# A selective-scan block on one core: sixteen copies of the B and C rows, last states that enter through the first token, and a shifted order of the next step's pieces

## The chip, the cores and the metric

The kernel runs on one core of a Trainium2 chip. The core has five engines that run their own instruction streams: TensorE (PE in the profile), VectorE (DVE), ScalarE (ACT), GpSimd (POOL) and SyncE (SP), which here only issues DMA transfers; 16 DMA engines move the data. The metric is the device time of one execution in microseconds. Before the change it is 13002.54 us, the median of three runs (12999.16 to 13004.72).

## The reference

Two images of 96 channels and 128 x 128 positions pass through two layers. Nearly all the work is in the first layer's mixer: four Mamba scans over the 16384 positions, in row order, reversed row order, column order and reversed column order. Cut to what matters, one direction is:

```
xc, z = split(x @ in_w.T)                       # 192 channels each
xc    = silu(causal_conv4(xc) + conv_b)
dt_raw, Bm, Cm = split(xc @ xproj_w.T)          # 6, 16 and 16 rows
dt    = softplus(dt_raw @ dt_w.T + dt_b)
for t in positions:                             # h: 192 channels x 16 states
    h = exp(dt[t] * A) * h + dt[t] * Bm[t] * xc[t]
    y[t] = sum over the states of h * Cm[t]
out   = ((y + Dp * xc) * silu(z)) @ outp_w.T
```

Bm and Cm have 16 rows each per position, common to all 192 channels of a direction. The four outputs are fused by a 1x1 product and added to x. After that come a quantized feed-forward part, a 3x3 convolution and a second feed-forward part, which the change doesn't touch.

## The kernel before

For each image three stages follow each other: `normalize` (layer norm, written to DRAM in row order and in column order), `mamba` (the four scans) and `ffn_and_conv`. The change is in `mamba` alone.

**Tiling.** Directions are taken in two pairs (`PAIRS`), first the two forward ones, then the two reversed. A pair has 2 x 192 = 384 channels, which make three groups `g` of 128 partitions: group 0 belongs to the first direction, group 2 to the second, and group 1 is half and half (partitions 0..63 first, 64..127 second). A *step* is one pair and one block of T = 512 positions; there are 2 x 32 steps per image, 128 in all. A step has 24 *units*: for each of three groups, eight pairs of states (`s`, `s+1`). The loop variable `k` counts units through all steps of an image, and in the text "unit 12" is the twelfth of its step.

**A unit.** ScalarE makes two decay tiles `da` = exp(dt * A) in PSUM (`decay`, L330, two units ahead). GpSimd multiplies the B rows by `dtu` = dt * xc in place (`b_part`, L324, also two units ahead; it covers two states at once, 1024 elements a partition). VectorE runs the recurrence over the 512 positions of each state (`scan`, L334), which starts from the state that the step before left in `hst`. It then multiplies the result by the C rows in one instruction of 1024 elements (L409). TensorE adds the products up over the states, as matrix products with the identity into `y` (`sums`, L341). ScalarE keeps the last column of `h` in `hst` (L410). VectorE's order is: first scan of unit k, product of unit k-1, second scan of unit k. At the first unit of a group the finished `y` of the group before is multiplied by silu(z) (`gated`, L349).

**Rows on all partitions.** A scan on 128 partitions needs each B and C row on every partition. `rows_out` (L258 to L261) copies B and C of a step from PSUM to SBUF (64 rows, on partitions 32 to 95, in the order B of the first direction, B of the second, C of the first, C of the second) and writes them to DRAM as `bcd`, in `COPIES` = 4 copies. `row_tile` (L312 to L321) then fetches four rows at a time, spread over the partitions by an access pattern with repeats, 8 KB a partition and 1 MB in all. For group 1 these are two transfers, one for each half of the partitions. A tile serves two units. There are four buffers for B and three for C, so that a transfer is issued when an older tile is done with: B for units k+6 and k+7 at the top of each even unit k (the buffer was read last by the scans of unit k-1), and C for units k+4 and k+5 at its end (read last by TensorE's sums of unit k-1). SyncE issues all transfers in the order of the program.

**Pieces of the next step.** While a step is scanned, the input of the next is prepared by small functions in `prologue`: `load`, three `conv` and `conv_out`, the silu of `xc`, three `gate` and `gate_out`, the silu of `sz`, `rows` and `rows_out`, and for each group the chain `dt_in`, `dt_exp`, `dt_ln`, `dt_q`, `dt_log`, `dt_sum`, `dt_u` (softplus by parts; `dt_q` to `dt_u` are four GpSimd operations of 512 elements, L287 to L297). Each has a place (unit, 0 or 1): 0 is ahead of the unit's first scan, 1 at its end. The list `at` holds these places. All engines run in the order in which the program issues (`manual_schedule`), so a piece that waits holds up everything behind it on its engine. The pieces' PSUM tile `misc` has one buffer.

Of the kernel before, what the change touches and what calls it, by code (L numbers as in the profile page):

```python
# [10 lines left out]
F32 = mybir.dt.float32  # L11
# [3 lines left out]
AF = mybir.ActivationFunctionType  # L15
ALU = mybir.AluOpType
# [7 lines left out]
T = 512  # L24
NT = L // T
R = T // W
S = 16
# [2 lines left out]
HID = 384  # L30
PAIRS = ((0, 2), (1, 3))
NG = 3
COPIES = 4
B_AHEAD = 3
C_AHEAD = 2
AHEAD = 2
# [1 line left out]
BCO = 32  # L38
NBC = 4 * S
# [3 lines left out]
def tile_metaformer(ctx: ExitStack, tc: tile.TileContext, a: dict, out: bass.AP):  # L43
# [139 lines left out]
    def mamba(acc, xnr, xnc):  # L183

        with ExitStack() as st:
# [3 lines left out]
            rows_d = pool("rows_d", 3, space=DRAM)  # L189

            hst = one.tile([128, NG, S], F32, name="hst")
            acc_w = acc.rearrange("c (h w) -> c w h", w=W)

            def misc():
# [15 lines left out]
            def prologue(pi, i, d):  # L210

                rev = pi == 1
                lo = L - (i + 1) * T if rev else i * T
                src = []

                def load():
                    for n, dram in (("xa", xnr), ("xb", xnc)):
                        t = io.tile([C, T + 3], F32, name=n)
                        if i == 0:
                            nc.gpsimd.memset(t[:, T : T + 3] if rev else t[:, 0:3], 0.0)  # L220
                            nc.sync.dma_start(t[:, 0:T] if rev else t[:, 3 : T + 3], dram[:, lo : lo + T])
                        else:
                            nc.sync.dma_start(t, dram[:, lo : lo + T + 3] if rev else dram[:, lo - 3 : lo + T])
                        src.append(t[:, ::-1] if rev else t)
                    d["dt"], d["dtu"], d["yg"] = [], [], []

                def conv(g):
                    d["ps"] = inproj(pi, g, lambda dd, k, lo, hi: inx[:, dd, k, lo:hi], src, (0, 1, 2, 3))

                def conv_out(g):  # L230
                    if g == 0:
                        d["xc"] = two.tile([128, NG, T], F32, name="xc")
                    nc.scalar.activation(d["xc"][:, g, :], d["ps"], AF.Identity, bias=convb[:, pi, g : g + 1])  # L233

                def gate(g):
                    d["ps"] = inproj(pi, g, lambda dd, k, lo, hi: inz[:, dd, lo:hi], src, (3,))

                def gate_out(g):
                    if g == 0:
                        d["sz"] = two.tile([128, NG, T], F32, name="sz")  # L240
                    nc.scalar.copy(d["sz"][:, g, :], d["ps"])

                def silu(name):
                    nc.scalar.activation(d[name], d[name], AF.Silu)
                    nc.scalar.preload_act_table_set("natural_log_exp_and_others")

                def rows():

                    d["ps"] = misc()
                    for g in range(NG):  # L250
                        nc.tensor.matmul(
                            d["ps"][0 : BCO + NBC, :], bcw[:, pi, g, :], d["xc"][:, g, :], start=g == 0, stop=g == NG - 1
                        )

                def rows_out():

                    d["rows"] = one.tile([BCO + NBC, T], F32, name="rows")
                    nc.scalar.copy(d["rows"], d["ps"][0 : BCO + NBC, :])  # L258
                    d["bcd"] = rows_d.tile([COPIES, 2, NBC // 2, T], F32, name="bcd")
                    for n in range(COPIES):  # L260
                        nc.sync.dma_start(d["bcd"][n].rearrange("k r t -> (k r) t"), d["rows"][BCO:, :])  # L261

                def dt_in(g):
                    d["ps"] = misc()
                    w = dtw[:, pi, g * 128 : (g + 1) * 128]
                    nc.tensor.matmul(d["ps"], w, d["rows"][0 : 2 * RK, :], start=True, stop=True)  # L268

                def dt_exp(g):  # L270
                    bias = dtb[:, pi, g : g + 1]
                    d["e"] = one.tile([128, T], F32, name="e")
                    nc.scalar.activation(d["e"], d["ps"], AF.Abs, bias=bias)
                    dt = gen.tile([128, T], F32, name="dt")
                    nc.scalar.activation(dt, d["ps"], AF.Relu, bias=bias)  # L275
                    nc.scalar.activation(d["e"], d["e"], AF.Exp, scale=-1.0)
                    d["dt"].append(dt)

                def dt_ln(g):
                    d["q"] = one.tile([128, T], F32, name="q")  # L280
                    nc.scalar.activation(d["q"], d["e"], AF.Identity, bias=1.0)
                    d["ln"] = one.tile([128, T], F32, name="ln")
                    nc.scalar.activation(d["ln"], d["q"], AF.Ln)
                    nc.scalar.activation(d["q"], d["q"], AF.Identity, bias=minus_one[:, 0:1])

                def dt_q(g):
                    nc.gpsimd.tensor_tensor(d["q"], d["e"], d["q"], ALU.subtract)  # L287

                def dt_log(g):
                    nc.gpsimd.tensor_tensor(d["ln"], d["ln"], d["q"], ALU.add)  # L290

                def dt_sum(g):
                    nc.gpsimd.tensor_tensor(d["dt"][g], d["dt"][g], d["ln"], ALU.add)  # L293

                def dt_u(g):
                    dtu = gen.tile([128, T], F32, name="dtu")
                    nc.gpsimd.tensor_tensor(dtu, d["dt"][g], d["xc"][:, g, :], ALU.mult)  # L297
                    d["dtu"].append(dtu)


                at = [(0, 0, load), (8, 1, partial(silu, "xc")), (14, 1, partial(silu, "sz"))]
                at += [(12, 0, rows), (12, 1, rows_out)]
                for g, k in enumerate((4, 5, 6)):
                    at += [(k, 0, partial(conv, g)), (k, 1, partial(conv_out, g))]
                for g, k in enumerate((7, 10, 11)):
                    at += [(k, 0, partial(gate, g)), (k, 1, partial(gate_out, g))]
                for g, k in enumerate((13, 18, 21)):
                    pieces = (0, 0, dt_in), (0, 1, dt_exp), (1, 1, dt_ln), (2, 0, dt_q), (3, 0, dt_log), (3, 0, dt_sum), (4, 0, dt_u)
                    at += [(k + m, where, partial(f, g)) for m, where, f in pieces]
                return sorted(at, key=lambda p: p[:2])  # L310

            def row_tile(d, g, s, k, ahead):  # L312

                t = gen.tile([128, 4, T], F32, name=f"row{k}", bufs=ahead + 1)
                for half in range(2) if g == 1 else (slice(None),):
                    rows = slice(half * 64, half * 64 + 64) if g == 1 else half
                    at = s + S * (half if g == 1 else g // 2)
                    n = (64 if g == 1 else 128) // COPIES
                    src = d["bcd"][None, :, k, at : at + 4, :].broadcast_to((n, COPIES, 4, T))
                    nc.sync.dma_start(t[rows], src)  # L320
                return t  # L321

            def b_part(d, g, b):
                nc.gpsimd.tensor_tensor(b, d["dtu"][g][:, None, :].broadcast_to((128, 2, T)), b, ALU.mult)  # L324

            def decay(pi, d, g, s):

# [2 lines left out]
                    nc.scalar.activation(da[:, j, :], d["dt"][g], AF.Exp, scale=amat[:, pi, g, s + j : s + j + 1])  # L330
                return da

            def scan(i, g, s, j, da, b, h):
                nc.vector.tensor_tensor_scan(  # L334
                    h[:, j, :], da[:, j, :], b[:, j, :],
                    0.0 if i == 0 else hst[:, g, s + j : s + j + 1], ALU.mult, ALU.add,
                )

            def sums(s, y, c):
                for j in range(2):  # L340
# [34 lines left out]
            def later(k, where, f, *args):  # L375
                todo.setdefault((k, where), []).append(partial(f, *args))
# [14 lines left out]
            def feed(k):  # L391
                if k < total:
                    n = k // nu
                    b_part(state[n], units[k % nu][0], bs[k])

            def feed_decay(k):
                if k < total:
# [38 lines left out]
            for k in range(total + 6):  # L436
                n, u = divmod(k, nu)
                if u == 0 and n + 1 < len(steps):
                    for m, where, f in prologue(*steps[n + 1], state[n + 1]):
                        later(k + m, where, f)  # L440
                if k % 2 == 0:
                    fetch(k + 2 * B_AHEAD, 0, B_AHEAD, bs)
                feed(k + AHEAD)
                issue(k, 0)
                if k < total:
                    (_, i), (g, s) = steps[n], units[u]
                    da, b = das.pop(k), bs.pop(k)
                    hs[k] = b if (g, s) in BY_POOL else da
                    scan(i, g, s, 0, da, b, hs[k])
                if 0 < k <= total:  # L450
                    behind(k - 1)
                if k < total:
                    scan(i, g, s, 1, da, b, hs[k])
                if k % 2 == 0:
                    fetch(k + 2 * C_AHEAD, 1, C_AHEAD, cs)
                feed_decay(k + AHEAD)
# [166 lines left out]
```

## Time and profile before

| What | us |
|---|---|
| span of the profiled execution | 13002.5 |
| scan stage of the first image (168.2 to 5932.9) | 5764.7 |
| scan stage of the second image (6660.5 to 12423.2) | 5762.7 |
| VectorE busy in each of them | 5489 |
| GpSimd busy in each | 4500 |
| ScalarE busy in each | 3864 |
| TensorE busy in each | 4816, 4806 |

The busy time of an engine over a stage tells how full it is; it doesn't tell which wait ends last. For that, the groups of instructions have a second time, the idle time of the engine ahead of them, and the engine or transfer that ended it. The waits of SyncE tell when a buffer became free for a transfer: 4676.5 us on TensorE's sums for the C tiles and 2049.5 us on the scans for the B tiles. The DMA queue moved 3394 MB, of which the row tiles are 24 MB a step; 512 transfers write `bcd`, 128 KB each, and they land 9.8 us after their issue in the median. A row transfer of 1 MB lands after 7.5 us in the median, one of 512 KB after 8.0.

### The profile page before, as it was taken

Reading aid. Unit: us, or ns where it says so; the run is one execution under the profiler, and the core shown is the slowest. Engines: PE = TensorE matmul, PEld = TensorE weight load, DVE = VectorE, ACT = ScalarE, POOL = GpSimd, SP = SyncE. Lnnn points to the kernel's source line nnn. Section 1 sums busy time; section 2 is a strip of 40 time slices with the busy share of each in tenths; the row PEclk is TensorE's granted clock in tenths of the full one; section 3 lists DMA queues with packets and bytes.
Section 4 is the critical chain, followed back from the end, with each engine's and each line's share of the span. In section 5 each row is a group of like instructions: output and inputs, shape, how many; then the busy total and the mean of one; then the engine's idle time right before and its main releaser. Section 6 shows DMA issues by size and latency. Waiting matters only on the chain. (4 is left out here: it accounts for less than half of the span.)

```text
span 13002.5 us, 97992 instructions
## 1 busy us (share of the span) xinstructions
PE 10850.3 (83%) x24208; PEld 3987.1 (31%) x24208; DVE 11569.1 (89%) x10865; ACT 8560.0 (66%) x14738; POOL 9215.4 (71%) x4772
## 2 busy tenths in 40 slices
PE   6888888888888888888978888888888888888889
PEld 2323233333333333333323333332333333333233
DVE  5999999999999999995459999999999999999954
ACT  6666666666666666665566666666666666666655
POOL 4877778777787787772147778777787777877721
PEclk8999999999999999999989999999999999999999
DMA  7999999999999999992079999999999999999920
GB/s 226 287 294 282 298 288 285 295 283 298 288 285 295 283 295 289 285 295 68 13 226 285 298 283 292 290 285 298 285 291 291 284 298 286 290 294 281 296 61 13
DMA packets 545331, 3400.40 MB, mean 262 GB/s; under 512 B 81612, under 2 KB 82732, under 8 KB 146840
## 3 DMA queue, kind: packets, MB, share of 16 engines
q1 hardware_dynamic: 544760, 3394.12, 83.1%
q8 instruction: 195, 3.19, 0.1%
q14 instruction: 376, 3.08, 0.1%
HBM read 3288.94 MB, written 104.86 MB: 261 GB/s over the span
## 5 line engine op out<-in xcount | busy, mean ns | idle before, releaser
L324 POOL TENSOR_TENSOR row<-dtu,row 128x1024 f32<-128x1024 f32 x3072 | 7175.7, 2358 | 1739.3 <-DMA row<-bcd 1419.2
L334 DVE TENSOR_TENSOR_SCAN da<-da,hst,row 128x512 f32<-128x512 f32 x5952 | 7339.4, 1274 | 351.2 <-ACT da L330 194.6
L341 PE MATMUL y<-row,ident 128*128 128x512 f32 x12288 | 6120.1, 626 | 1113.3 <-DVE row L409 1098.9
L330 ACT ACTIVATE da<-dt,amat 128x512 f32<-128x512 f32 x6144 | 4249.4, 692 | 207.5 <-ACT hst L410 0.4
L341 PEld LDWEIGHTS y<-row,ident 128*128 128x128 f32 x12288 | 2288.9, 197 | 4779.4 <-DVE row L409 2292.3
L409 DVE TENSOR_TENSOR row<-da,row 128x1024 f32<-128x1024 f32 x3072 | 3705.9, 1206 | 19.6 <-DMA row<-bcd 18.8
L410 ACT COPY hst<-da 128x2 f32<-128x2 f32 x3072 | 484.0, 158 | 2235.5 <-DVE row L409 2233.3
L416 PE MATMUL y<-xc,dmat 128*128 128x512 f32 x768 | 526.1, 773 | 779.1 <-DVE sz L349 779.1
L287 POOL TENSOR_TENSOR q<-e,q 128x512 f32<-128x512 f32 x384 | 488.0, 1271 | 821.8 <-ACT hst L410 709.1
L233 ACT ACTIVATE xc<-misc,convb 128x512 f32<-128x512 f32 x384 | 264.2, 688 | 1117.5 <-PE misc L207 1117.5
L207 PE MATMUL misc<-xa,inx 96*128 96x512 f32 (+1 forms) x2048 | 932.4, 597 | 59.0 <-DMA xa<-xnr 57.2
L207 PE MATMUL misc<-xb,inx 96*64 96x512 f32 (+1 forms) x2048 | 928.1, 595 | 1.6 <-ACT xc L233 1.6
L531 POOL TENSOR_TENSOR acc<-acc,y 96x512 f32<-96x512 f32 x128 | 147.6, 1153 | 987.0 <-DVE y L530 987.0
L541 PE MATMUL pc<-pad,kw 96*96 96x512 f32 x1152 | 566.7, 593 | 0.0
L207 PEld LDWEIGHTS misc<-xa,inx 96*128 96x128 f32 (+1 forms) x2048 | 323.6, 163 | 625.5 <-issue 493.4
L293 POOL TENSOR_TENSOR dt<-dt,ln 128x512 f32<-128x512 f32 x384 | 486.9, 1268 | 30.1
L297 POOL TENSOR_TENSOR dtu<-dt,xc 128x512 f32<-128x512 f32 x384 | 488.5, 1272 | 0.5
L290 POOL TENSOR_TENSOR ln<-ln,q 128x512 f32<-128x512 f32 x384 | 488.1, 1271 | 0.5
L359 PE MATMUL misc<-sz,gmat 128*96 128x512 f32 x1024 | 483.6, 594 | 0.0
L416 PEld LDWEIGHTS y<-xc,dmat 128*128 128x128 f32 x768 | 129.0, 211 | 1102.1 <-DVE sz L349 1099.1
L268 PE MATMUL misc<-rows,dtw 12*128 12x512 f32 x768 | 439.7, 652 | 18.5 <-ACT dt L275 17.2
L132 DVE TENSOR_TENSOR xq<-xm,rs 96x512 fp8e5<-96x512 f32 x128 | 87.9, 687 | 387.8 <-ACT rs L128 387.8
(75 smaller groups left out, 8403.8 us busy)
## 6 DMA issues: line engine op xcount, KB each, us to landing
row<-bcd SPq DMA_DIRECT2D x2048, 1024.0 KB, 7.5
row<-bcd SPq DMA_DIRECT2D x2048, 512.0 KB, 8.0
bcd<-rows SPq DMA_DIRECT2D x512, 128.0 KB, 9.8
xa<-xnr SPq DMA_DIRECT2D x124, 193.1 KB, 5.8
xb<-xnc SPq DMA_DIRECT2D x124, 193.1 KB, 5.5
acc<-in_x_dram SPq DMA_DIRECT2D x16, 768.0 KB, 17.8
xnr<-xn SPq DMA_DIRECT2D x16, 768.0 KB, 4.3
xnc<-stg SPq DMA_DIRECT2D x16, 768.0 KB, 5.6
```

The source lines that it names most:

```text
L207: nc.tensor.matmul(ps[rows, :], w(PAIRS[pi][d], k, lo, hi), src[d][:, k : k + T], **se)
L287: nc.gpsimd.tensor_tensor(d["q"], d["e"], d["q"], ALU.subtract)
L290: nc.gpsimd.tensor_tensor(d["ln"], d["ln"], d["q"], ALU.add)
L293: nc.gpsimd.tensor_tensor(d["dt"][g], d["dt"][g], d["ln"], ALU.add)
L297: nc.gpsimd.tensor_tensor(dtu, d["dt"][g], d["xc"][:, g, :], ALU.mult)
L324: nc.gpsimd.tensor_tensor(b, d["dtu"][g][:, None, :].broadcast_to((128, 2, T)), b, ALU.mult)
L330: nc.scalar.activation(da[:, j, :], d["dt"][g], AF.Exp, scale=amat[:, pi, g, s + j : s + j + 1])
L334: nc.vector.tensor_tensor_scan(h[:, j, :], da[:, j, :], b[:, j, :], 0.0 if i == 0 else hst[:, g, s + j : s + j + 1], ALU.mult, ALU.add,)
L341: nc.tensor.matmul(y, ident, c[:, j, :], start=False, stop=s + j == S - 1)
L409: nc.vector.tensor_tensor(c, h, c, ALU.mult)
L416: nc.tensor.matmul(y, dmat[:, pi, g, :], d["xc"][:, g, :], start=True, stop=False)
L541: nc.tensor.matmul(pc, kw[:, t, :], rows, start=t == 0, stop=t == 8)
```

## The change

Three things are done together.

1. **Rows.** `bcd` gets 16 copies of each direction's rows instead of four copies of all, and its layout puts the two directions' copies one after the other, with a pad of one row between copies. A tile of group 1 can then be read as one transfer over 128 partitions (copies 8 to 23: half of them the first direction's, half the second's). The copies are written by four transfers, one for each set of 16 rows, each with a repeat over the copies; the writing is a piece of its own, `rows_to_dram`.
2. **States.** A scan now always starts from the constant 0. What the last state adds, decay times state at the first position, is put into the first column of the B part instead: `entering` computes exp(A * dt at the first position) * `hst` for a whole group (16 states), one ScalarE and one GpSimd operation, four units ahead of the group's first unit, and `b_part` adds two columns of it to the first tokens of its two states with a GpSimd operation of its own. In the first block of a pair there is no state, and nothing is added.
3. **Places.** The pieces of the next step are moved: convolutions from units 4, 5, 6 to 3, 5, 6 with their copies out a whole unit later instead of in the same one; gates from 7, 10, 11 to 9, 10, 11, copied out half a unit later; the silu of `sz` from 14 to 12; the dt chains from 13, 18, 21 to 14, 17, 20, each stretched by about a unit.

```diff
-COPIES = 4
+COPIES = 16
...
+            enter = one.tile([128, NG, S], F32, name="enter")
...
                 def rows_out():
-
                     d["rows"] = one.tile([BCO + NBC, T], F32, name="rows")
                     nc.scalar.copy(d["rows"], d["ps"][0 : BCO + NBC, :])
-                    d["bcd"] = rows_d.tile([COPIES, 2, NBC // 2, T], F32, name="bcd")
-                    for n in range(COPIES):
-                        nc.sync.dma_start(d["bcd"][n].rearrange("k r t -> (k r) t"), d["rows"][BCO:, :])
+
+                def rows_to_dram():
+
+                    d["bcd"] = rows_d.tile([2, 2 * COPIES, S + 1, T], F32, name="bcd")
+                    for n in range(4):
+                        to = d["bcd"][n // 2, n % 2 * COPIES : (n % 2 + 1) * COPIES, 0:S, :]
+                        r = d["rows"][BCO + n * S : BCO + (n + 1) * S, None, :].broadcast_to((S, COPIES, T))
+                        nc.sync.dma_start(to.rearrange("n s t -> s n t"), r)
...
-                at = [(0, 0, load), (8, 1, partial(silu, "xc")), (14, 1, partial(silu, "sz"))]
-                at += [(12, 0, rows), (12, 1, rows_out)]
-                for g, k in enumerate((4, 5, 6)):
-                    at += [(k, 0, partial(conv, g)), (k, 1, partial(conv_out, g))]
-                for g, k in enumerate((7, 10, 11)):
-                    at += [(k, 0, partial(gate, g)), (k, 1, partial(gate_out, g))]
-                for g, k in enumerate((13, 18, 21)):
-                    pieces = (0, 0, dt_in), (0, 1, dt_exp), (1, 1, dt_ln), (2, 0, dt_q), (3, 0, dt_log), (3, 0, dt_sum), (4, 0, dt_u)
+                at = [(0, 0, load), (8, 1, partial(silu, "xc")), (12, 1, partial(silu, "sz"))]
+                at += [(12, 1, rows), (13, 0, rows_out), (13, 1, rows_to_dram)]
+                for g, (k, where) in enumerate(((3, 1), (5, 0), (6, 1))):
+                    at += [(k, where, partial(conv, g)), (k + 1, where, partial(conv_out, g))]
+                for g, k in enumerate((9, 10, 11)):
+                    at += [(k, 1, partial(gate, g)), (k + 1, 0, partial(gate_out, g))]
+                for g, k in enumerate((14, 17, 20)):
+                    pieces = (0, 1, dt_in), (1, 0, dt_exp), (1, 1, dt_ln), (3, 0, dt_q), (4, 0, dt_log), (4, 0, dt_sum), (5, 0, dt_u)
                     at += [(k + m, where, partial(f, g)) for m, where, f in pieces]
...
             def row_tile(d, g, s, k, ahead):
 
                 t = gen.tile([128, 4, T], F32, name=f"row{k}", bufs=ahead + 1)
-                for half in range(2) if g == 1 else (slice(None),):
-                    rows = slice(half * 64, half * 64 + 64) if g == 1 else half
-                    at = s + S * (half if g == 1 else g // 2)
-                    n = (64 if g == 1 else 128) // COPIES
-                    src = d["bcd"][None, :, k, at : at + 4, :].broadcast_to((n, COPIES, 4, T))
-                    nc.sync.dma_start(t[rows], src)
+
+                src = d["bcd"][k, COPIES // 2 * g : COPIES // 2 * g + COPIES, None, s : s + 4, :]
+                nc.sync.dma_start(t, src.broadcast_to((COPIES, 128 // COPIES, 4, T)))
                 return t
 
-            def b_part(d, g, b):
+            def entering(pi, d, g):
+
+                nc.scalar.activation(enter[:, g, :], amat[:, pi, g, :], AF.Exp, scale=d["dt"][g][:, 0:1])
+                nc.gpsimd.tensor_tensor(enter[:, g, :], enter[:, g, :], hst[:, g, :], ALU.mult)
+
+            def b_part(i, d, g, s, b):
                 nc.gpsimd.tensor_tensor(b, d["dtu"][g][:, None, :].broadcast_to((128, 2, T)), b, ALU.mult)
+                if i > 0:
+                    nc.gpsimd.tensor_tensor(b[:, :, 0], b[:, :, 0], enter[:, g, s : s + 2], ALU.add)
...
-            def scan(i, g, s, j, da, b, h):
-                nc.vector.tensor_tensor_scan(
-                    h[:, j, :], da[:, j, :], b[:, j, :],
-                    0.0 if i == 0 else hst[:, g, s + j : s + j + 1], ALU.mult, ALU.add,
-                )
+            def scan(j, da, b, h):
+                nc.vector.tensor_tensor_scan(h[:, j, :], da[:, j, :], b[:, j, :], 0.0, ALU.mult, ALU.add)
...
                     for m, where, f in prologue(*steps[n + 1], state[n + 1]):
                         later(k + m, where, f)
+                    if steps[n + 1][1] > 0:
+                        for g in range(NG):
+                            later(k + nu - 4 + nu // NG * g, 1, entering, steps[n + 1][0], state[n + 1], g)
```

More of the change, by code (lines that the diff above doesn't have):

```diff
@@ L393, in feed @@
                     n = k // nu
-                    b_part(state[n], units[k % nu][0], bs[k])
+                    b_part(steps[n][1], state[n], *units[k % nu], bs[k])
             def feed_decay(k):
@@ L445, in mamba @@
                 if k < total:
-                    (_, i), (g, s) = steps[n], units[u]
+                    (g, s) = units[u]
                     da, b = das.pop(k), bs.pop(k)
                     hs[k] = b if (g, s) in BY_POOL else da
-                    scan(i, g, s, 0, da, b, hs[k])
+                    scan(0, da, b, hs[k])
                 if 0 < k <= total:
@@ L452, in mamba @@
                 if k < total:
-                    scan(i, g, s, 1, da, b, hs[k])
+                    scan(1, da, b, hs[k])
                 if k % 2 == 0:
```

## The prediction

> **What bounds it now.** The page first: VectorE (DVE) is full in both stretches of the scan stage, and the 16 DMA engines nearly so.
>
> ```profile
> DVE  5999999999999999995459999999999999999954
> DMA  7999999999999999992079999999999999999920
> ...
> L324 POOL TENSOR_TENSOR row<-dtu,row 128x1024 f32<-128x1024 f32 x3072 | 7175.7, 2358 | 1739.3 <-DMA row<-bcd 1419.2
> L334 DVE TENSOR_TENSOR_SCAN da<-da,hst,row 128x512 f32<-128x512 f32 x5952 | 7339.4, 1274 | 351.2 <-ACT da L330 194.6
> ```
>
> The windows give 11527.4 us for the two scan stages (168.2 to 5932.9, 6660.5 to 12423.2), 90.06 us for each of 128 steps of 24 units; all else takes 1475 us. A unit is two scans and one 1024-wide product. The timeline of VectorE shows its beat, with the last state as a scan's start (first lines) and with the constant 0 of a first step (last two):
>
> ```profile
> 3037.16 1.21 DVE L409 TENSOR_TENSOR row<-da,row 128x1024 f32<-128x1024 f32 x1
> 3040.64 1.21 DVE L409 TENSOR_TENSOR row<-da,row 128x1024 f32<-128x1024 f32 x1
> ...
> 3058.37 1.21 DVE L409 TENSOR_TENSOR row<-da,row 128x1024 f32<-128x1024 f32 x1
> ...
> 3061.73 1.21 DVE L409 TENSOR_TENSOR row<-da,row 128x1024 f32<-128x1024 f32 x1
> ```
>
> 3.48 us against 3.36. So 24 x 3.487 + 3 x 0.6 (the gate, L349) = 85.5 us of a step is VectorE's work. The other 4.6 us are waits: for ScalarE's decay factors (about 1.6 us at unit 9, 1.4 at unit 17) and for TensorE's y (171 us over 128 steps, 1.3 each). Waits for rows were 19 us in all: the transfers are late for nobody yet.
>
> How near they are, the windows tell by GB/s (last column, after the DMA share):
>
> ```profile
> 2994.00:3004.00 10.00, 9.22 (x23) 3.25 (x22) 8.68 (x9) 9.51 (x14) 4.65 (x2) 1.00 1.01 222
> 3022.00:3032.00 10.00, 6.02 (x9) 2.53 (x10) 8.73 (x9) 6.26 (x13) 8.54 (x6) 0.72 1.03 426
> 71.30:74.50 3.20, 3.20 (x9) 1.23 (x8) 1.37 (x2) 3.14 (x7) 0.00 (x0) 1.00 0.81 246
> ```
>
> In the first the group g=1 is fetched, in transfers to 64 partitions: 222 GB/s with every engine busy. In the second come transfers to 128 partitions: 426 GB/s. The third is one store from 96 partitions, alone on the engines: 246. A full row transfer thus takes 2.5 us, a half one 2.4 for half the bytes.
>
> [...]
>
> **The change, part by part.** Times are per step; T12 is the start of unit 12.
>
> 1. Scans start from 0: 24 x (3.487 - 3.364) = 3.0 us off the bound engine. VectorE's work becomes 82.5 us.
>
> 2. The state enters through `b`'s first token: 24 adds of 128x2 on GpSimd and 3 products of 128x16, with 3 exponentials on ScalarE, which has room (67% in the stage). No such narrow operation is in the trace. From 2358 at 1024 and 1271 at 512 the fixed part is 184 ns; that is my lower end, 300 the upper. The add waits for the product before it; the same wait between L290 and L293 makes their distance 1.35 us where others have 1.22. I take 0.27 us per unit. GpSimd then needs 24 x 2.58 + 12 x 1.26 + 0.6 = 77.6 us, below 82.5, but it comes in a burst: the pieces of three groups (5.03 us each) fall before units 18 to 28. Today's burst is just on time:
>
> ```profile
> 3056.84 1.27 POOL L293 TENSOR_TENSOR dt<-dt,ln 128x512 f32<-128x512 f32 x1
> 3058.06 2.35 POOL L324 TENSOR_TENSOR row<-dtu,row 128x1024 f32<-128x1024 f32 x1
> 3060.37 1.27 POOL L297 TENSOR_TENSOR dtu<-dt,xc 128x512 f32<-128x512 f32 x1
> 3061.60 9.30 POOL L324 TENSOR_TENSOR row<-dtu,row 128x1024 f32<-128x1024 f32 x4
> ```
>
> The product for unit 27 ends at 3060.4, its scan begins at 3060.6; unit 28's ends at 3063.9, its scan at 3064.0.
>
> 3. Group 1's two half transfers become one full: 16 x 2.4 - 8 x 2.5 = 18.4 us less DMA work.
>
> 4. Four copies of 128 KB from 64 partitions (about 1.2 us together) become four transfers of 512 KB, each from 16 partitions. [...]at the full 420 GB/s it would be 5.0. I take 20.2[...]. The sum of DMA work stays near 81 us (24 x 2.5 + 20.2 + 1), but 20.2 us of it is now one block in which no row arrives. Behind the four on SyncE's queue stand B for units 20-21 and C for 18-19.
>
> Walk it. ScalarE copies `rows` out after the silu (L244, table loads included 4.05 us) of slot (12,1): T12 + 8.7. With 1.3 us to start, the block runs from T12 + 10.0 to 30.2; B for unit 20 lands at 33.2 (2.5 us, 0.5 to signal), C for unit 18 at 35.7. (1.3 and 0.5 are my split of the 1.8 us by which the quickest row landing, 4.3, exceeds its 2.5.) VectorE would need C at 25.3: it stops some 10 us. GpSimd starts unit 20 only at 33.2, and the burst follows: nine products with adds (9 x 2.58 = 23.2), log, sum and u of group 0 (3.8), two whole groups (10.1), one entering product (0.2): 37.3 us. Unit 28 can't be scanned before T12 + 70.5. Undisturbed it would be at 16 x 3.364 + 2 x 0.6 = 55.0. The loss is 15.5 us, the 10 us included. From unit 28 to 36 GpSimd needs 2.58 against 3.36 and recovers its lead, so each step repeats it.
>
> 5. The pieces move. The silu of `sz` (4.05) and `dt_ln` (2.0) no longer meet in slot (14,1), and a convolution is copied out one unit after it is issued, not in the same one, so ScalarE doesn't stand waiting for TensorE (1117 us at L233). I take both ScalarE waits as gone: 2.9 us. The wait for y stays at 1.3, since projection and three convolutions still queue ahead of that gate.
>
> 6. At each image's start the first rows wait for the block: 2 x 19 us; the last step of each image has no next step's block, 2 x 15.5 less. These cancel within 10 us.
>
> **Sum.** 82.5 + 15.5 + 1.3 = 99.3 us a step; 128 x 99.3 + 1475 = 14,190 us, 9% slower.
>
> **Rivals.**
>
> *The block is short* (reads at the full rate, 5.0 us). For it: two thirds of the packets of that store took 309 ns per 8 KB, as quick as those of the full row transfers. Against: the others took up to three times that, and the whole ran at 246 GB/s. B for unit 20 then lands at T12 + 18.0, and GpSimd is held only by the entering product at unit 20, which waits for ScalarE until T20 + 4.2 = 31.7; from there 0.2 + 6 x 2.58 + 3.8 + 5.0 gives unit 28 at 56.2, 1.2 us late. 82.5 + 1.2 + 1.3 = 85.0; 12,360 us, faster.
>
> *Halved block*: [...]10.1 us. B lands at 23.1, unit 28 at 60.4, 5.4 us late: 89.2 us, 12,890 us. Against it: halves in today's trace don't overlap.
>
> *Only the lead is used up*: the rows' lead hides the block. Today it hides group 1's deficit, four pairs of tiles at 9.6 us of transfers per 7.0 of VectorE, 10.4 us. The walk already grants C a lead of 10 us from its landing without the block (about T12 + 15.5); 20.2 us is beyond that. A part of it would give some 93 us a step, 13,380 us.
>
> **Chances.** The long block 0.80, with the last rival inside its spread; short 0.14; halved 0.06. Within the first, 21.5 us of block (a 2 KB packet of `bcd` takes 84 ns in the trace[...]) and 0.3 us more per add give +1.3 and +3 us a step, 14,700; a block of 15 us and more lead take 6 to 9 off, down to about 13,100. The range from 12,880 to 14,700 leaves out the short block, a part of the halved one and few of the first: about 0.2. Faster 0.18 (the short and most of the halved), same 0.02, slower 0.80.
>
> **What would show it.** Right: L334 without `hst` at 1214 ns; [...]VectorE's product (L415 in the new numbering) waiting for rows about 10 us a step; scans waiting for GpSimd at units 24 to 28; landings of `bcd` from 10 to some 25 us. Wrong: `bcd` transfers at 200 GB/s or more, or no wait of VectorE for rows; then the step is near 85 us. If the rows wait but GpSimd doesn't, the burst's term is too large.

## The result and the profile after

The changed kernel takes 15249.52 us (median of four runs, 15222.82 to 15256.42) against 13002.48: the ratio is 1.1725, with a 95% interval from 1.1704 to 1.1745. The direction was forecast, the size was not: 14,190 was predicted, and 14,700 was the end of the range.

Read as before, first the slices and the groups that answer to those of the prediction (in a group: busy us and mean ns, then the idle time ahead of it and what ended most of it), then the transfers with their size and median landing:

```profile
DVE  4778777777777777776447877877777778877864
DMA  8999999999999999995079999999999999999940
...
L331 POOL TENSOR_TENSOR row<-dtu,row 128x1024 f32<-128x1024 f32 x3072 | 7225.0, 2352 | 3793.4 <-DMA row<-bcd 3482.0
L343 DVE TENSOR_TENSOR_SCAN da<-da,row 128x512 f32<-128x512 f32 x6144 | 7181.7, 1213 | 216.1 <-POOL row L331 84.5
L415 DVE TENSOR_TENSOR row<-da,row 128x1024 f32<-128x1024 f32 x3072 | 3731.6, 1215 | 2977.5 <-DMA row<-bcd 2963.0
...
L333 POOL TENSOR_TENSOR row<-row,enter 128x2 f32<-128x2 f32 x2976 | 577.3, 194 | 233.4
...
row<-bcd SPq DMA_DIRECT2D x3072, 1024.0 KB, 19.0
bcd<-rows SPq DMA_DIRECT2D x512, 512.0 KB, 13.6
```

In the kernel before, the product by C read:

```profile
L409 DVE TENSOR_TENSOR row<-da,row 128x1024 f32<-128x1024 f32 x3072 | 3705.9, 1206 | 19.6 <-DMA row<-bcd 18.8 <-DVE da L334 0.4
```

VectorE's line fell from nines to sevens and eights; the DMA line stayed at nines. The scan is cheaper, as meant (1213 ns; 1274 before). But VectorE now stands idle for rows 2963 us ahead of the product by C, where it stood 18.8 us before, and a row transfer lands after 19.0 us instead of 7.5. The two scan stages, by window (the last two columns are DMA share and GB/s):

```profile
166.20:7088.20 6922.00, 5235.03 (x10559) 1895.62 (x10560) 5361.91 (x4798) 3926.11 (x6867) 4822.09 (x3967) 0.90 1.01 255
7815.80:14674.00 6858.20, 5229.65 (x10559) 1883.38 (x10560) 5363.36 (x4799) 3923.37 (x6867) 4821.32 (x3968) 0.90 1.01 258
```

They add up to 13780.2 us, 107.7 for a step instead of 90.06. All 16 DMA engines are busy throughout, and move only 255 GB/s, when 24 full transfers a step were each to run at some 420. The bound has moved from VectorE to the DMA engines. The packets (the pieces into which a transfer is divided) say how: a row packet of 8 KB takes 521 ns in the mean, 541 in the median. Before, one of a full transfer took 309 to 312 ns in the median, one of a half transfer 612. A step has 24 x 8 row packets for each engine: 192 x 0.521 = 100 us. Add the writing of `bcd` (64 packets of 2 KB at 0.100) and the inputs, and the step is full.

VectorE's timeline shows a long stop, and behind it a short one at every second product, which is every new C tile (idle time in brackets):

```profile
2310.47 1.22 DVE L415 TENSOR_TENSOR row<-da,row 128x1024 f32<-128x1024 f32 x1 [11.29 <-DMA row<-bcd]
...
2313.86 1.21 DVE L415 TENSOR_TENSOR row<-da,row 128x1024 f32<-128x1024 f32 x1
...
2319.17 1.23 DVE L415 TENSOR_TENSOR row<-da,row 128x1024 f32<-128x1024 f32 x1 [1.85 <-DMA row<-bcd]
...
2327.93 1.22 DVE L415 TENSOR_TENSOR row<-da,row 128x1024 f32<-128x1024 f32 x1 [1.93 <-DMA row<-bcd]
```

The first of these lines is the product of unit 18 (units count from 0), where the prediction had put the stop behind the long writes. Counted through the whole run, this product waits for rows in each of the 128 steps: 879 us, 6.9 a step. The rest of the 2963 us, 16.3 a step, is spread over the other C tiles: 3.6 us at unit 4, and 0.2 to 1.7 at each of the others.

### The profile page after: what moved, and what is told of

It is laid out like the page before. It is cut to its first block, busy times and chain, and to the rows that moved or that the text cites. A ratio compares the mean times of both kernels' runs of the same rounds, so it can differ in the third digit from the quotient of the medians.

```text
span 15250.7 us, 99404 instructions
## 1 busy us (share of the span) xinstructions
PE 11691.6 (77%) x24208; PEld 4248.7 (28%) x24208; DVE 11315.7 (74%) x10865; ACT 8680.1 (57%) x15110; POOL 9858.8 (65%) x8120
## 5 line engine op out<-in xcount | busy, mean ns | idle before, releaser
L347 PE MATMUL y<-row,ident 128*128 128x512 f32 x12288 | 6858.6, 693 | 2157.6 <-DVE row L415 2127.0
L343 DVE TENSOR_TENSOR_SCAN da<-da,row 128x512 f32<-128x512 f32 x6144 | 7181.7, 1213 | 216.1 <-POOL row L331 84.5
L347 PEld LDWEIGHTS y<-row,ident 128*128 128x128 f32 x12288 | 2502.5, 217 | 6385.7 <-DVE row L415 3819.5
L422 PE MATMUL y<-xc,dmat 128*128 128x512 f32 x768 | 560.3, 819 | 1041.2 <-DVE sz L355 1041.2
L208 PE MATMUL misc<-xa,inx 96*128 96x512 f32 (+1 forms) x2048 | 994.6, 630 | 203.3 <-DMA xa<-xnr 168.5
L278 ACT ACTIVATE e<-misc,dtb 128x512 f32<-128x512 f32 x384 | 263.8, 687 | 884.6 <-PE misc L273 699.5
L333 POOL TENSOR_TENSOR row<-row,enter 128x2 f32<-128x2 f32 x2976 | 577.3, 194 | 233.4
L286 ACT ACTIVATE q<-e 128x512 f32<-128x512 f32 x384 | 239.5, 624 | 595.8 <-POOL ln L295 594.9
L242 ACT COPY sz<-misc 128x512 f32<-128x512 f32 x384 | 225.2, 586 | 586.6 <-PE misc L208 586.0
## 6 DMA issues: line engine op xcount, KB each, us to landing
bcd<-rows SPq DMA_DIRECT2D x512, 512.0 KB, 13.6
xa<-xnr SPq DMA_DIRECT2D x124, 193.1 KB, 20.2
```

Of the source, the lines that this page charges most:

```text
L208: nc.tensor.matmul(ps[rows, :], w(PAIRS[pi][d], k, lo, hi), src[d][:, k : k + T], **se)
L333: nc.gpsimd.tensor_tensor(b[:, :, 0], b[:, :, 0], enter[:, g, s : s + 2], ALU.add)
L343: nc.vector.tensor_tensor_scan(h[:, j, :], da[:, j, :], b[:, j, :], 0.0, ALU.mult, ALU.add)
L347: nc.tensor.matmul(y, ident, c[:, j, :], start=False, stop=s + j == S - 1)
L422: nc.tensor.matmul(y, dmat[:, pi, g, :], d["xc"][:, g, :], start=True, stop=False)
```

## The experiments

Two questions were open: what makes the row packets slow, and what the rest of the change is worth. The change to the rows has three parts that can each be at fault: that 16 copies are **written** (2 MB a step from 16 partitions at a time), that they lie in many **places** which are read once each (H in the expectations), or the **shape** of the reading (S in the expectations): the transfer names 16 blocks of eight partitions, each block from one copy, where it named 32 blocks of four before, the four copies in turn. The times are ratios to the kernel before, each with its 95% interval.

### The rows as before, the rest kept (e1_old_rows)

```diff
-COPIES = 16
+COPIES = 4
...
-                    for n in range(4):
...
+                    for n in range(COPIES):
+                        nc.sync.dma_start(d["bcd"][n].rearrange("k r t -> (k r) t"), d["rows"][BCO:, :])
...
+                for half in range(2) if g == 1 else (slice(None),):
...
+                    src = d["bcd"][None, :, k, at : at + 4, :].broadcast_to((n, COPIES, 4, T))
```

> The changed kernel with its row part taken back: four copies written from 64 partitions, group 1 fetched in two half transfers, as before; entering states and new places stay. Both theories of the slow rows (S: a full transfer whose source is cut in 16 blocks of 8 partitions is slow, one cut in 32 blocks of 4 is not; H: the engines are slow[...]) expect rows as fast as before: 222 and 420 GB/s. VectorE then has 82.5 us of work a step, waits for y 1.3 us and for GpSimd's burst 1 to 3 us: 85 to 88 us a step, 12360 to 12740 us. If the entering adds or the places were a cause of the loss, it stays above 13000.

12766.4 us, ratio 0.9819 (0.9803 to 0.9835). So the whole loss comes from the rows, and the states and the places together gain 236 us, a little less than expected. No kernel measured here is faster; e7 below equals it. A step takes 88.2 us. VectorE's waits (us in total, times, longest):

```profile
DVE da L344 <- POOL row L334: 255.4, 311, 1.6
DVE sz L356 <- PE y L348: 214.9, 138, 2.5
```

The entering adds hold scans for 2.0 us a step, 1.4 of it at unit 3; the wait for y has grown from 171 to 215 us, 1.7 a step. VectorE is busy for 83.3 us of the step (10661.9 us over the two scan stages), and these two waits are 3.7 of the other 4.9.

### Sixteen copies written, three ways to read them (e2_fours, e3_eights, e4_read_old)

The writing stays that of the change in all three. e2 reads blocks of four, still in single transfers to 128 partitions; e3 reads blocks of eight in groups 0 and 2, eight copies in turn instead of 16; e4 reads exactly as the kernel before did.

```diff
-                src = d["bcd"][k, COPIES // 2 * g : COPIES // 2 * g + COPIES, None, s : s + 4, :]
-                nc.sync.dma_start(t, src.broadcast_to((COPIES, 128 // COPIES, 4, T)))
+# e2
+                if g == 1:
+                    src = d["bcd"][k, :, None, s : s + 4, :].broadcast_to((2 * COPIES, 4, 4, T))
+                else:
+                    src = d["bcd"][None, k, COPIES // 2 * g : COPIES // 2 * g + 4, s : s + 4, :].broadcast_to((32, 4, 4, T))
+# e3, groups 0 and 2
+                    src = d["bcd"][None, k, c0 : c0 + 8, s : s + 4, :].broadcast_to((16, 8, 4, T))
+# e4, in halves for group 1
+                    src = d["bcd"][None, k, c0 : c0 + 4, s : s + 4, :].broadcast_to((n, 4, 4, T))
```

> The changed kernel, its writing kept, with the source of a row transfer cut in 32 blocks of 4 partitions: groups 0 and 2 read four copies in turn, group 1 reads all 32 copies, each for four partitions; all are single transfers over 128 partitions. S expects every tile at about 2.5 us, so DMA work of some 67 us a step, no waits for rows, 84 to 86 us a step: 12230 to 12500 us. H expects groups 0 and 2 at 2.5 us and group 1 as slow as now (4.2 us): rows of group 1 late, 12500 to 13000 us. If the write block is the cause, over 13500 us.

> The changed kernel with groups 0 and 2 reading eight copies in turn: 16 blocks of 8 partitions as in the changed kernel, but [...]only eight places are read; group 1 as in the changed kernel. S expects all tiles to stay slow, about 525 ns a packet of 8 KB, and 15000 us or more. H expects groups 0 and 2 at about 312 ns and group 1 at 525: DMA work 16 x 2.5 + 8 x 4.2 + 7.4 = 81 us a step, 12500 to 13000 us.

> The changed kernel with 16 copies written, read as before: four copies in turn, two half transfers for group 1. Against the first kernel of this call it differs by the writing alone: 1024 packets of 2 KB a step instead of 256. If these run at their 84 to 100 ns it is 6.4 us of DMA work instead of 1.6: 86 us of DMA work a step, 12700 to 13200 us. If the block holds the queue for 20 us as the prediction had it, 13500 us or more.

e2 took 13799.97 us, 1.0613 (1.0597 to 1.0629); e3 15339.11, 1.1796 (1.1770 to 1.1822); e4 14169.43, 1.0897 (1.0875 to 1.0919).

The row packets give a clear verdict: 309 ns in the median and 348 in the mean in e2, 547 and 526 in e3, with fewer places than the change has. It is the shape. Blocks of four against blocks of eight is 1450 us between e2 and the changed kernel, 11.3 a step. e3's window of the first image has the same two marks as the changed kernel's, a full share and 254 GB/s:

```profile
163.60:7133.80 6970.20, 5294.07 (x10559) 1907.64 (x10560) 5364.13 (x4798) 3927.47 (x6867) 4816.30 (x3967) 0.89 1.01 254
```

But e2 was expected at some 12,230 to 12,500 on this theory and missed that by far. What is left is the writing. e2's windows around one step's writing, before, in and after it:

```profile
2230.00:2238.00 8.00, 7.18 (x18) 2.68 (x18) 8.00 (x8) 6.11 (x13) 0.72 (x2) 1.00 0.93 356
2245.50:2259.50 14.00, 9.87 (x21) 3.47 (x22) 14.00 (x14) 9.78 (x19) 7.30 (x7) 1.00 0.91 180
2262.00:2270.00 8.00, 2.92 (x6) 1.04 (x5) 3.22 (x3) 1.09 (x2) 5.51 (x5) 0.81 1.01 422
```

In the third the rows run at 422 GB/s. In the second the engines are nearly as busy (0.91), and move 180, some packets of other transfers included. The four writes of 512 KB take 16.2 us in the median of the 128 steps (here from 2244.1 to 2260.1, with 0.65 MB of other packets among them). A written packet of 2 KB takes 186 ns in the mean; a quarter take 84, another quarter 295 and more. VectorE comes through the block and then stands where the prediction had put it, at the product of unit 18 (first line), and a scan some units later waits for GpSimd (second):

```profile
2266.78 1.23 DVE L418 TENSOR_TENSOR row<-da,row 128x1024 f32<-128x1024 f32 x1 [6.62 <-DMA row<-bcd]
...
2285.43 1.23 DVE L346 TENSOR_TENSOR_SCAN da<-da,row 128x512 f32<-128x512 f32 x1 [1.43 <-POOL row L336]
```

Over the whole run, the first of these happens once in each of the 128 steps:

```profile
DVE row L418 <- DMA row<-bcd: 830.6, 128, 8.0
DVE da L346 <- POOL row L336: 377.4, 372, 1.8
```

That is 6.5 and 2.9 us a step, and a step of 96.4 us. e4 against e1 differs by the writing, and by the layout in DRAM that goes with it, alone: 1403 us. There the same wait for rows is 1198.0 us, 9.4 a step. That it is longer than in e2 because the halves of group 1 leave a smaller lead is likely, but no run isolates it.

### The block made short (e7_short_block)

This is e2 with four copies written instead of 16, by the same four transfers from 16 partitions each. All groups read those four in turn; half of group 1 thereby gets the other direction's rows, so that its values differ while its transfers are the same.

```diff
-                        to = d["bcd"][n // 2, n % 2 * COPIES : (n % 2 + 1) * COPIES, 0:S, :]
-                        r = d["rows"][BCO + n * S : BCO + (n + 1) * S, None, :].broadcast_to((S, COPIES, T))
+                        to = d["bcd"][n // 2, n % 2 * COPIES : n % 2 * COPIES + 4, 0:S, :]
+                        r = d["rows"][BCO + n * S : BCO + (n + 1) * S, None, :].broadcast_to((S, 4, T))
...
-                src = d["bcd"][k, COPIES // 2 * g : COPIES // 2 * g + COPIES, None, s : s + 4, :]
-                nc.sync.dma_start(t, src.broadcast_to((COPIES, 128 // COPIES, 4, T)))
+                src = d["bcd"][None, k, COPIES // 2 * g // 16 * 16 : COPIES // 2 * g // 16 * 16 + 4, s : s + 4, :].broadcast_to((32, 4, 4, T))
+                nc.sync.dma_start(t, src)
```

> The kernel that cuts the source in 32 blocks of 4, with only four copies of each direction written, still from 16 partitions (256 packets instead of 1024); all groups read four copies in turn, and the second half of group 1 gets the first direction's rows, which changes that part of the result. The long block (16.2 us measured, VectorE waits 6.5 us at unit 18's product and then for GpSimd at units 23 and 24) becomes 4 to 5 us. If the block is the whole difference between 13800 and the kernel with the old rows, the time is that of the latter, 12700 to 12800 us; if single full transfers for group 1 gain something, less, down to 12500.

12774.1 us, 0.9824 (0.9804 to 0.9844). The block is 3.3 us in the median, VectorE has no wait for rows in its list any more, and the 1026 us between e2 and this kernel are the long block's. The second finding lies in what did not happen. Group 1 is read here in full transfers, rows land after 5.4 us in the median (7.5 for full and 8.6 for half transfers in e1), GpSimd's idle time for rows falls from 678.8 us in e1 to 28.5, and the time is the same as e1's. What holds VectorE is the same as there:

```profile
DVE da L343 <- POOL row L333: 266.1, 346, 1.6
```

So the single transfers that the many copies were for had nothing to give in this kernel: nobody on the path was waiting for group 1.

### How many places, how large a block (e12_small_blocks, e8_ports)

e12 is e2 with still smaller blocks: in group 0 two copies in turn, in group 2 one copy for all 128 partitions.

```diff
-                    src = d["bcd"][None, k, COPIES // 2 * g : COPIES // 2 * g + 4, s : s + 4, :].broadcast_to((32, 4, 4, T))
+                    m = 2 if g == 0 else 1
+                    src = d["bcd"][None, k, COPIES // 2 * g : COPIES // 2 * g + m, s : s + 4, :].broadcast_to((128 // m, m, 4, T))
```

> The kernel that cuts the source in blocks of four and writes 16 copies, with group 0 read in 64 blocks of two (two copies in turn) and group 2 from a single copy for all 128 partitions; group 1 in 32 blocks of four. If only blocks larger than four are slow, all tiles stay at about 310 ns a packet and the time at 13800 us. If few places in DRAM are slow, group 2 (one place) is the slowest, and the time rises above 14000 us.

13776.6 us, 1.0597 (1.0576 to 1.0619), row packets of 309 ns in the median and 345 in the mean: practically the same as e2. One place in DRAM serves all 128 partitions as fast as four do (e2: 309 and 348 ns).

e8 keeps the blocks of eight partitions but cuts the transfer into pieces, so that fewer blocks are under way at once: four transfers of four blocks in group 0, two of eight in group 2, one of 16 in group 1. It takes much longer, with the DMA engines busy half of the time ("5" in nearly every slice of the DMA line); only its packets count here.

```diff
+                parts = (4, 1, 2)[g]
+                n, m = 128 // parts, COPIES // parts
+                for p in range(parts):
+                    src = d["bcd"][k, c0 + m * p : c0 + m * (p + 1), None, s : s + 4, :]
+                    nc.sync.dma_start(t[n * p : n * (p + 1)], src.broadcast_to((m, 8, 4, T)))
```

> A look at packets alone; it will be much slower. The changed kernel, with group 0's tile fetched in four transfers of 32 partitions, each from four copies with eight partitions a copy; group 2's in two transfers of 64 partitions, each from eight copies with eight partitions a copy; group 1 as in the changed kernel.[...] If eight partitions from one copy are slow in themselves, group 0's packets are slow too, 500 ns or more.

23661.29 us, one run. The packets are sorted by how many are under way at once, taken as the number of busy engines. With four, an 8 KB packet takes 309 ns in the median (309 to 318 from the 5th to the 95th percentile), with eight 311 (a quarter above some 380, 5% above some 610), with 16 605. So a block of eight from one copy isn't slow in itself; it is slow when 16 of them run together (605 ns). Which engine serves which partitions is not in the records, so what slows the 16 stays open. What is shown is the effect of the cut as a whole. Whether it is the eight partitions of a block or the number of 16 blocks isn't separated, since in a full transfer the one fixes the other; the half transfers of the kernel before, 16 blocks of four on 64 partitions, were slow too (612 ns in the median).

### The two other parts, each alone on the kernel before (e9_entering, e10_places)

```diff
+# e9: the states enter through the first token, places as before
+                nc.vector.tensor_tensor_scan(h[:, j, :], da[:, j, :], b[:, j, :], 0.0, ALU.mult, ALU.add)
...
+# e10: the list of places of the change; scans still start from hst
+                at += [(12, 1, rows), (13, 0, rows_out), (13, 1, rows_to_dram)]
```

> The kernel before with part 2 alone: states enter through the first token, rows and places as before. If the prediction's terms are right, scans give back 3.0 us a step, while GpSimd's burst, just on time before, is late by 11 adds of 0.27 us, 3 us: no gain, 12900 to 13200 us, with scans waiting for GpSimd at units 26 to 28. If the adds are hidden, 12620 us.

> The kernel before with part 3 alone: the new places. By the prediction ScalarE's two waits (2.9 us a step) go and the wait for y (1.3 us) stays: 87.2 us a step, 12640 us. If the waits only move to y or to GpSimd, 12850 to 13000 us.

e9: 13065.02 us, 1.0050 (1.0033 to 1.0066). e10: 12805.11 us, 0.9851 (0.9836 to 0.9866). The first line is e9's, the second e10's:

```profile
DVE da L342 <- POOL row L332: 391.2, 611, 1.6
```

```profile
DVE sz L350 <- PE y L342: 273.0, 135, 2.5
```

The cheaper scans alone gain nothing, and the kernel is some 60 us slower: the 3.0 us that VectorE saves in a step are spent on waits for GpSimd's adds (391.2 us, 3.1 a step), and most of the old waits for ScalarE remains (254.5 us of 338.8). The places alone gain 197 us. The waits of scans for ScalarE leave the list, and part of what they cost comes back as a longer wait for y. Together with the states (e1) it is 236 us: the two parts don't simply add.

### Can the two waits that are left be moved? (e5_late_chain, e6_late_early, e11_projection)

e5 and e11 start from e1, e6 from e5. e5 puts the dt chain of group 2 at units 8 to 13 of its own step, out of GpSimd's burst. e6 adds earlier convolutions, to empty TensorE's queue ahead of the gate that waits for y, which runs at unit 9. e11 instead moves the output projection of group 2 behind the sums that this gate waits for.

```diff
+# e5
-                for g, k in enumerate((14, 17, 20)):
+                for g, k in enumerate((14, 17, 32)):
-                    pieces = (0, 1, dt_in), (1, 0, dt_exp), (1, 1, dt_ln), (3, 0, dt_q), (4, 0, dt_log), (4, 0, dt_sum), (5, 0, dt_u)
+                    pieces = (0, int(g < 2), dt_in), (1, 0, dt_exp), (1, 1, dt_ln), (3, 0, dt_q), (4, 0, dt_log), (4, 0, dt_sum), (5, 0, dt_u)
+# e6, on e5
-                for g, (k, where) in enumerate(((3, 1), (5, 0), (6, 1))):
+                for g, (k, where) in enumerate(((2, 0), (4, 0), (5, 1))):
+# e11, for g == 2
-                    later(k + 4, 0, project, pi, i, d, g)
+                        later(k + 9, 1, project, pi, i, d, g)
```

> The kernel with the rows as before (entering states and new places kept) and group 2's dt chain moved from units 20-25 to units 8-13 of its own step, where its first scan is at unit 16. Theory of the burst (GpSimd is late at units 0 to 4 because three groups' chains fall before them): the waits of scans for GpSimd, 299 us for b and enter, go down to under 50 and the time to some 12480 to 12560 us. If GpSimd were short of time over the whole step instead, the waits only move and the time stays near 12766.

> The same with the three convolutions about a unit earlier (2, 4, 5 and a half instead of 3 and a half, 5, 6 and a half), so that TensorE has done its queue before the gate at unit 9. If the wait for y (1.3 to 1.8 us a step) comes from convolutions and projection queued ahead of it, it falls below 0.5 us a step and the time by another 130 to 220 us, to 12270 to 12430 us. If y is late for another reason the time equals that of the kernel before it in this call.

> The kernel with the old rows, entering states and new places, with group 2's projection moved from unit 3 of the next step to the end of unit 8, behind the sums that the gate at unit 9 waits for. If that gate's wait for y (1.7 to 1.8 us a step) is three products of the projection in front of TensorE's queue, it goes: 12500 to 12580 us, unless GpSimd's burst (2.4 us a step at units 3, 4 and 24), which overlaps nothing now, grows by as much; then the time stays at 12766.

e5: 12811.84 us, 0.9854 (0.9839 to 0.9869). e6: 13093.84, 1.0072 (1.0055 to 1.0089). e11: 12935.25, 0.9951 (0.9936 to 0.9965). None beats e1. e5 does what it was made for, the scans' waits for the adds fall from 255.4 to 34.5 us, and the wait for y takes the time instead:

```profile
DVE sz L356 <- PE y L348: 472.2, 129, 3.8
...
DVE da L344 <- POOL row L334: 34.5, 121, 0.3
```

So e5's expected gain did not come, and neither did e6's. There the wait for y falls from e5's 472.2 us to 226.3, which is about e1's again, while scans wait for ScalarE (357.7 us) and products for rows (172.7 us):

```profile
DVE da L344 <- ACT hst L417: 357.7, 366, 2.4
DVE sz L356 <- PE y L348: 226.3, 132, 2.1
DVE row L416 <- DMA row<-bcd: 172.7, 125, 3.2
```

e11's expectation failed too. The wait for y stayed what it was, so the projection isn't what it waits for, and scans now wait for ScalarE (276.6 us in all, where e1 has 39.7), which the moved piece must have held up:

```profile
DVE sz L356 <- PE y L348: 212.9, 135, 2.4
...
DVE da L344 <- ACT hst L417: 170.4, 124, 1.7
```

What does hold y at that gate wasn't isolated.

## Why the prediction was right or wrong, step by step

- **Step 1, scans from 0: right.** 1213 ns were measured where 1214 had been read off the first steps of the kernel before.
- **Step 2, the adds: right in size.** 577.3 us busy and 233.4 of idle time ahead of them, over 2976 adds, is 0.27 us each, the value taken. The burst that it feeds was right in place and too large: 5.5 us a step had been worked out on top of the stop for C, and in e2 scans wait for GpSimd 2.9, at units 24, 27 and 28. Of these, e1 has 2.0 without any long block, so that the block adds only 0.9.
- **Step 3, the rows: the step that failed.** It priced 24 full row transfers at 2.5 us each, because the trace before showed 2.5 for a transfer to 128 partitions. That price belongs to a transfer cut into blocks of four, and the change altered the cut together with the number of transfers. With 521 ns a packet, eight packets for each engine are 4.2 us: 24 x (4.2 - 2.5) = 41 us of DMA work a step that the sum did not have. The writes in turn needed 6.4 us instead of 20.2, so that the 81 us of the sum become 108, and 107.7 us is the measured step. With that the DMA engines need more than VectorE's 82.5 us and become the bound. The prediction looked at the destination's partitions and at the source of the writes, and took the source of the reads as free; no rival had slower rows, so the range could not hold the time.
- **Step 4, the long block: right in kind, its size too large.** The 20.2 us were the author's estimate; the trace before, in which `bcd` is written from 64 partitions, shows no such time. With fast rows (e2) the block is 16.2 us, about 129 GB/s (2.1 MB in 16.2 us), and costs VectorE 6.5 us of waiting where some 10 had been worked out. In the changed kernel the stop stands at the same product, 6.9 us a step. The other marks named in "what would show it" for the block are missing there: the scans' waits for the adds are 28.4 us in the whole run, and `bcd` lands after 13.6 us where some 25 had been forecast. The writes are mixed with rows there (11.5 us in the median of the steps, with 1.6 MB of other packets among them, and 100 ns a packet in the mean) and make no stretch of their own. That few partitions make a write slow was not shown when the prediction was made. The runs agree in the main: the same 512 KB take 3.3 us when they are written from 16 partitions (e7, with 0.1 MB of other packets among them), and 2.4 us from 64 (e1, with about 0.5 MB). But the cost of a packet also changes with what lies between the writes (100 ns in the mean in the changed kernel, 186 in e2), so the partitions alone don't set it.
- **Step 5, the places: half right.** The waits for ScalarE go, as said (e10), though they were 2.6 us a step (338.8 / 128) and not 2.9, and behind the long block 1.4 us of them are back (e2). The wait for y does not stay at 1.3 us a step: it becomes 2.1 in e10 (273.0 / 128) and 1.7 in e1. The step gained 1.5 us where 2.9 were taken.
- **The rivals.** "The block is short" was put at 12,360; made true in e7, it came to 12774.1, since 85.0 us a step left out the growth of the wait for y and the waits for the adds at unit 3. Its argument, two thirds of a store's packets at 309 ns, was misread: in the store shown it is 36 of 96, with 50 under 340. "Halved block" was not what happened (10.1 us were taken, 16.2 measured in e2); that halves don't overlap is in the trace before, where those of group 1 land one after the other, 2.3 to 2.4 us apart (four of them from 2997.9 to 3005.0). "Only the lead is used up", at 93 us a step, was nearer to e2 than "halved" and about as far from it as the main case.
- **What was luck.** That the change would be slower was not: the block that was foreseen makes e2 6% slower than the kernel before. But e2's 96.4 us a step stands near the forecast 99.3 in part because errors cancel: the stop and the burst are 9.4 us instead of 15.5, while VectorE's work (83.6 instead of 82.5), the wait for y (1.9 instead of 1.3) and the waits for ScalarE (1.4 instead of none) are larger.

The account of the 2247 us, from the pairs of kernels: places -197 (e10), states on top of them -39 (e1 against e10), single transfers for group 1 about +8 (e7 against e1), the long writes +1026 (e2 against e7), the blocks of eight +1450 (the changed kernel against e2). The shares belong to this order of the steps: blocks of eight with a short block were not run, and where the DMA engines are the bound the writes may cost another amount.

## What to carry to other kernels

When a change rewrites the access pattern of a transfer, its price must be measured anew, for both sides of the pattern: same bytes, same 128 partitions and same destination gave 348 or 521 ns a packet in the mean (309 or 541 in the median) by the cut of the source alone. Before transfers are made cheaper, see whether anything on the path waits for them: here 18.8 us in 13,002 did, and what pays for the cheaper reads (four times the bytes written, from 16 partitions at a time) was a block in front of the rows. And where engines run in a fixed order with little lead over the bound one, a saving there tends to come back as a wait: in e9 3.1 us a step of waits for GpSimd took the 3.0 saved, in e5 the wait for y rose from 214.9 to 472.2 us, in e11 scans waited 276.6 us for ScalarE instead of 39.7, and none made the kernel faster than what it started from.

## What was not expected of the hardware

- A transfer of 1 MB from DRAM to 128 partitions runs at some 420 GB/s when its source is named as 32 blocks of four partitions (422 in e2's window, 309 ns for each 8 KB in the median), and its packets take as long with 64 blocks of two or 128 of one (309 ns over all rows of e12). Where it is named as 16 blocks of eight, the engines are as full and move some 250 (254 in e3's window, 255 and 258 in those of the changed kernel; 521 to 526 ns for each 8 KB in the mean). With only four such blocks at once (e8) the 309 ns are back.
- The number of copies in DRAM doesn't matter for the reading: one place for all 128 partitions (e12, group 2) is as fast as two or four (345 ns in the mean over e12's rows, 348 in e2).
- Writes of 2 KB packets out of 16 partitions take 84 ns in the median and 100 in the mean in the changed kernel, where slow row packets lie between them, but 160 and 186 in e2, where they stand together in one block. That they are cheaper with slow packets between them was not expected, and no run isolates why.
